# Other slots for the parts of two selective-scan layers, and a third buffer for `du`

## The chip, the cores and the metric

The kernel runs on one core of one Trainium2 chip. The metric is the device time of one execution in microseconds, lower is better; times are medians of several runs. Five queues issue the work: TensorE (PE; its weight loads are shown apart as PEld), VectorE (DVE), ScalarE (ACT), GpSimd (POOL) and SyncE (SP, which here issues nearly all DMAs). Each queue runs its instructions in the order in which the program wrote them, and instructions on different queues wait for each other through semaphores.

## The reference

Two layers follow each other on an image of 64 by 64 pixels and 192 channels, batch 8. Each normalises its input in groups, projects it to 384 channels for `x` and 384 for the gate `z`, applies a 3 by 3 depthwise convolution and SiLU, and runs a selective scan along the pixels in K directions (K = 2 in layer 0: rows forward and backward; K = 4 in layer 1: rows and columns, both ways). The sum over the directions is normalised over the channels, multiplied by the gate and projected back. Of each layer this matters:

```python
xs = ...                                              # [B, K, 384, 4096]
x_dbl = jnp.einsum('bkdl,kcd->bkcl', xs, x_proj_weight)
dts, Bs, Cs = jnp.split(x_dbl, [DT_RANK, DT_RANK + D_STATE], axis=2)
delta = jax.nn.softplus(jnp.einsum('bkrl,kdr->bkdl', dts, dt_projs_weight) + bias)
# for every pixel t, with 16 states n per channel:
#   h = exp(delta * A) * h + (delta * x) * B ;  y = sum_n h * C
y = (sum of the directions + x * Ds)
y = (y - mean) * rsqrt(var + eps) * ln_w + ln_b
out = einsum(y * act(z), out_proj_w)                  # act: gelu in layer 0, silu in layer 1
x = x + out
```

All arithmetic is float32.

## The kernel before

**Tiling.** The 384 channels are three tiles of 128 partitions (`DT` = 3, index `dt`), the 4096 pixels eight chunks of 512 (`T`). For each layer, `front` makes the convolved `x` of all images and leaves it in HBM; then `scans` does the rest. `scans` is what the change touches.

**Steps and slots.** A step `i` is one chunk of one direction `k` of one image: 128 steps in layer 0, 256 in layer 1. A step has 24 slots: slot `s` handles the state pair `m = s // 3` (two of the 16 states) and the channel tile `dt = s % 3`. In each slot the main loop writes, in this order:

- `scan` (L459): two hardware scans on DVE (L475), one for each state, which read `hb` from PSUM and `da`, and one multiplication of 1024 elements per partition on POOL, `hc = h * cr` (L476);
- the parts that a table `todo` holds for this slot;
- `inject(g + 2)` (L424): 8 matrix products that make `hb = delta * x * B` for the slot after the next. `hb` has two buffers of two PSUM banks each, so `inject(g + 2)` can start only when the scans of slot `g` have read theirs;
- `decay(g + 4)` (L444): two exponentials on ACT that make `da` for four slots on. `da` has five buffers, so this waits for the scans of slot `g - 1`.

So all queues are held to the pace of the scan pairs, PE two slots ahead and ACT four.

**The parts.** `at(i, s, f, ...)` puts part `f` at slot `s` of step `i`; numbers below 0 or above 23 fall in earlier or later steps. Within a slot, parts are sorted by `rank_of`: `f_keep`, then `f_act`, then the rest, then the products that use the buffer "m", then `reduce` and `add_y`, then loads. Three kinds of parts are put there.

- For the next step: `load_x`; in layer 1 `x_proj` (three products into `pd`) and `x_dbl`, in layer 0 `load_xdbl`; `turn_b` and `keep_b` (B is turned and sent to HBM); for each `dt`, `dt_proj` (PE, `pt`) and `dt_bias` (ACT, into `delta`); then `dt_softplus` (ACT, with a table load before and after it), and for each `dt` `make_du` (DVE, L383: `du = delta * x`, all operands in SBUF), `turn_du` (PE, `pq`) and `keep_du` (ACT).
- For the step itself: `load_b`, `load_c` (SP); `carry` (ACT); `reduce(m, n)` (PE: 12 products that add `hc` of one state to `py`); `load_y` or, where the direction changes from columns to rows, `load_turned` in 12 pieces; `add_y` (PE: 12 products that add y of the directions before); `keep_y` (ACT: copies `py` to SBUF, then five stores).
- For the chunks whose directions are all done, spread over K steps from step `e` on ("finish"): `f_norm`, `f_gate`, `f_keep` (the gate); `f_sum`, `f_keep_sum`, `f_all` (a mean over channels on PE, ACT, PE), `f_center` (DVE), `f_square` (ACT), the same three for the variance, `f_rstd` (ACT), `f_scale` (DVE), `f_act` (ACT), `f_affine` (ACT), `f_times` (POOL), `f_out` (PE), `f_add` (DVE), `f_store`. In layer 0, `e` is an odd step and the work covers that and the next (even) one; in layer 1 it covers four.

The last image's chunks can't wait for later steps; they get a denser order of their own in the last steps of a layer (`f_mean` in place of `f_sum` and `f_all`).

**One buffer for many.** PSUM has eight banks: four for `hb`, three for `py`, and one, the tag "m", which `pd`, `pb`, `pt`, `pq`, `pz`, `ps`, `pm` and `po` share. So a product that writes a new one of these waits until ACT or DVE has read the one before. In SBUF, `y` (for `load_y`, `load_turned` and the output of `keep_y`) has one buffer too, `du` has two, `h` two and `hc` and `cr` three.

Of the kernel before, what the change touches and what calls it, by code (L numbers as in the profile page):

```python
# [8 lines left out]
F32 = mybir.dt.float32  # L9
# [34 lines left out]
L0_ORDER = [1, 0]  # L44
L1_DIRS = [(True, False), (True, True), (False, True), (False, False)]
L1_ORDER = [1, 3, 2, 0]


def softplus(nc, out, in_):
# [200 lines left out]
            x_proj(*last)  # L250


def scans(tc, name, x_src, x_dst, xcd, xcd_col, xdd, t, dirs, rank, row_b, gate, consts, dram):

# [30 lines left out]
    with tc.tile_pool(name=f"{name}_s1", bufs=1) as s1, tc.tile_pool(  # L287
# [78 lines left out]

        def dt_bias(i, dt):
            k = steps[i][1]
            if dt == 0:
                live[i]["delta"] = s2.tile([P, DT, T], F32, name="delta")  # L370
            nc.scalar.activation(  # L371
                live[i]["delta"][:, dt], live[i]["pt"], AF.Identity, bias=dtb[:, k, dt : dt + 1]
            )
# [5 lines left out]

        def make_du(i, dt):  # L380

            du = s2.tile([P, T], F32, name="du")
            nc.vector.tensor_mul(  # L383
                du.rearrange("p (g r j) -> p r g j", r=2, j=G),
                live[i]["delta"][:, dt].rearrange("p (r g j) -> p r g j", r=2, j=G),
                live[i]["x"][:, dt].rearrange("p (r g j) -> p r g j", r=2, j=G),
            )
            live[i]["du", dt] = du
# [5 lines left out]
            live[i]["pq"] = pq  # L394

        def keep_du(i, dt):
            if dt == 0:
                live[i]["dut"] = s2.tile([P, DT, GC, P], F32, name="dut")
            nc.scalar.copy(live[i]["dut"][:, dt], live[i]["pq"])  # L399

# [145 lines left out]
        def f_norm(b, c):  # L546
            xn = s1.tile([P, DT, T], F32, name="xn_sq")
            fin["xn"] = xn[:CP, :CT]
            for u in range(CT):
                nc.scalar.activation(  # L550
                    fin["xn"][:, u],
                    fin["x"][:, u],
                    AF.Identity,
                    bias=t["gnb"][:, b, u : u + 1],
                    scale=t["grs"][:, b, u : u + 1],
                )
# [11 lines left out]
                )  # L568

        def f_keep(dt):  # L570
            if dt == 0:
                fin["g"] = s1.tile([P, DT, T], F32, name="g")
            nc.scalar.copy(fin["g"][:, dt], fin["pz"])

# [79 lines left out]
            )  # L654

        for i in range(N):
            j = i - 1  # L660
            at(j, -8, load_x, i)
            if xdd is None:
                for dt, s in enumerate((0, 1, 3)):
                    at(j, s, x_proj, i, dt)
                at(j, 4, x_dbl, i)
                b0, pts, act, d0 = 5, (6, 7, 9), 11, 13
            else:
                at(j, -4, load_xdbl, i)
                b0, pts, act, d0 = 2, (3, 4, 6), 9, 12
            at(j, b0, turn_b, i)  # L670
            at(j, b0 + 1, keep_b, i)
            for dt, s in enumerate(pts):
                at(j, s, dt_proj, i, dt)
                at(j, s + 1, dt_bias, i, dt)
            at(j, act, dt_softplus, i)
            for dt in range(DT):
                at(j, d0 + dt, make_du, i, dt)
                at(j, d0 + dt + 1, turn_du, i, dt)
                at(j, d0 + dt + 2, keep_du, i, dt)
            at(i, -12, load_b, i, 0)  # L680
            at(i, 0, load_b, i, 1)
            for m in range(NP):
                at(i, 3 * m - 6, load_c, i, m)
                at(i, 3 * m + 3, carry, i, m)
                for n in range(2):
                    at(i, 3 * m + 5 + n, reduce, i, m, n)
            b, k, cols, rev, ci, c = steps[i]
            if k and dirs[k - 1][0] != cols:
                for j in range(4 * DT):
                    at(i, 8 + j, load_turned, i, j)  # L690
                at(i, 24, add_y, i)
            else:
                at(i, 8, load_y, i)
                at(i, 15, add_y, i)
            at(i, 28, keep_y, i)

        def dealt(e, s, f, *a):

            for p, q in enumerate(s):
                at(e, q, f, *a, p)  # L700

        e = 0
        for b in range(B - 1):
            for c in range(NCH):
                e = max(e + K, (b + 1) * K * NCH - NCH + c + 1)
                if K == 2:
                    at(e, 0, f_load_x, b, c)
                    at(e, 6, f_load, b, c)
                    at(e, 6, f_norm, b, c)
                    for dt, s in enumerate(((7, 9), (16, 18), (19, 21))):  # L710
                        dealt(e, s, f_gate, dt)
                        at(e, s[1] + 1, f_keep, dt)
                    at(e, 22, f_sum, "y")
                    at(e, 23, f_keep_sum)
                    at(e, 24, f_all, "pm")
                    at(e, 25, f_center)
                    at(e, 26, f_square)
                    at(e + 1, 7, f_sum, "sq")
                    at(e + 1, 8, f_keep_sum)
                    at(e + 1, 10, f_all, "pv")  # L720
                    at(e + 1, 9, f_act)
                    at(e + 1, 11, f_rstd)
                    at(e + 1, 12, f_scale)
                    dealt(e + 1, (13, 14, 15), f_affine)
                    dealt(e + 1, (14, 15, 16), f_times)
                    for u, s in enumerate(((17, 18, 19), (20, 21, 22))):
                        dealt(e + 1, s, f_out, u)
                        at(e + 1, s[2] + 1, f_add, u)
                    at(e + 1, 23, f_store, b, c)
                else:  # L730
                    at(e, 0, f_load_x, b, c)
                    at(e, 6, f_load, b, c)
                    at(e, 8, f_norm, b, c)
                    for dt, s in enumerate(((10, 12), (18, 19), (21, 22))):
                        dealt(e, s, f_gate, dt)
                        at(e, s[1] + 1, f_keep, dt)
                    at(e + 1, 18, f_sum, "y")
                    at(e + 1, 19, f_keep_sum)
                    at(e + 1, 21, f_all, "pm")
                    at(e + 1, 22, f_center)  # L740
                    at(e + 1, 23, f_square)
                    at(e + 2, 11, f_act)
                    at(e + 2, 18, f_sum, "sq")
                    at(e + 2, 19, f_keep_sum)
                    at(e + 2, 21, f_all, "pv")
                    at(e + 2, 22, f_rstd)
                    at(e + 2, 23, f_scale)
                    dealt(e + 3, (6, 7, 8), f_affine)
                    dealt(e + 3, (7, 8, 9), f_times)
                    for u, s in enumerate(((10, 11, 12), (18, 19, 21))):  # L750
                        dealt(e + 3, s, f_out, u)
                        at(e + 3, s[2] + 1, f_add, u)
                    at(e + 3, 22, f_store, b, c)

        m0 = 10 if xdd is None else 7
        for c in range(NCH):
            b, e = B - 1, N - NCH + c + 1
            at(e, 5, f_load_x, b, c)
            at(e, 5, f_load, b, c)
            at(e, m0 + 4, f_norm, b, c)  # L760
            at(e, m0, f_mean, "y", "pm", 0, 1, 2)
            at(e, m0 + 1, f_center)
            at(e, m0 + 1, f_square)
            at(e, m0 + 2, f_mean, "sq", "pv", 0, 1, 2)
            at(e, m0 + 3, f_rstd)
            at(e, m0 + 4, f_scale)
            for dt in range(DT):
                at(e, m0 + 5, f_affine, dt)
                at(e, 17 + dt, f_gate, dt, 0, 1)
                at(e, 18 + dt, f_keep, dt)  # L770
                at(e, 20 + dt, f_times, dt)
            at(e, 20, f_act)
            for u in range(CT):
                at(e, 22 + u, f_out, u, 0, 1, 2)
                at(e, 23 + u, f_add, u)
            at(e, 24, f_store, b, c)

        rank_of = {
            f: r
# [23 lines left out]
                g += 1  # L803


def vss_layer(tc, name, x_src, x_dst, w, dirs, rank, row_b, gate, consts, dram):

    with ExitStack() as ctx:
        xcd, xcd_col, xdd, *dram = dram
# [3 lines left out]
            xcd_col = None  # L813
        t = load_weights(tc, ctx, name, w, len(dirs), rank, row_b + 2 * NS, consts[1])
        front(tc, name, x_src, xcd, xcd_col, xdd, t, consts)
        scans(tc, name, x_src, x_dst, xcd, xcd_col, xdd, t, dirs, rank, row_b, gate, consts, dram)


@with_exitstack
def two_vss_layers(ctx, tc, x, grp_d, w0, w1, out):  # L820
# [32 lines left out]
        for d in dgd:  # L853
            nc.sync.dma_start(out=d.rearrange("e (p x) -> (e p) x", p=P // 2), in_=zero)
    dram = (xcd, xcd_col, xdd, yrow, ycol, cscr, dgd)
    vss_layer(tc, "l0", x, mid, w0, L0_DIRS, 12, 32, AF.Gelu, consts, dram)
    vss_layer(tc, "l1", mid, out, w1, L1_DIRS, 96, 96, AF.Silu, consts, dram)


# [55 lines left out]
```

## Time and profile before

| | us |
|---|---|
| median of 3 runs | 27002.46 (26998.01 to 27004.6) |
| the profiled execution itself | 26994.35 |
| its span, from the first to the last instruction | 26992.1 |
| first scan and end of the scans of layer 0 | 1149.5 and 9797.8 |
| first scan and end of the scans of layer 1 | 10862.4 and 26916.4 |
| mean granted TensorE clock | 0.977 |

A page of the profile gives for each engine the time in which it was busy. A row of the costliest groups has the line, the engine, the operation, the tile written and the tiles read with their shapes and how often; then busy time in us and the mean of one in ns; then the idle time of the engine just before these instructions and what ended most of it. A timeline line has the start and the length in us, the engine, the line, what was written from what, and how many instructions were merged; in brackets the idle time before and what ended it. Lines with SPq are DMA issues on SyncE's queue: the length is that of the issue, the transfer lands later. Some groups that the change moves:

| line | what | count | mean ns |
|---|---|---|---|
| L434 | one of the 16 recorded products of an `inject` | 147456 | 289 |
| L451 | one exponential of `decay` | 18432 | 714 |
| L383 | `make_du` | 1152 | 887 |
| L50 | softplus over 1536 elements | 384 | 1485 |
| L524 | `keep_y` | 384 | 1439 |
| L633 | `f_times` | 384 | 1276 |
| L605, L616 | `f_center`, `f_scale` | 128 each | 1732, 1742 |
| L648 | `f_add` | 256 | 664 |

### The profile page before, as it was taken

What the parts mean: (1) busy time and instruction counts of PE and PEld (TensorE: products, weight loads), DVE (VectorE), ACT (ScalarE), POOL (GpSimd) and SP (SyncE); (2) the same over time, 40 slices, a digit from 0 to 9 for tenths busy, and PEclk for the clock granted to TensorE, in tenths of its full rate; (3) what the DMA queues carried; (4) which work ended last, traced back from release to release, by engine and by line L of the source; (5) the groups of instructions that cost most, each with busy time, mean ns of one, the idle gap of its engine ahead of it and who ended that gap; (6) DMA issues with size and microseconds to landing.
All of it is one profiled execution on the core that took longest, in us unless ns stands there. A gap on an engine that the chain in (4) does not pass through costs nothing.

```text
span 26992.1 us, 801807 instructions
## 1 busy us (share of the span) xinstructions
PE 24824.5 (92%) x348800; PEld 13646.4 (51%) x348800; DVE 23761.3 (88%) x21018; ACT 17601.2 (65%) x28132; POOL 23023.0 (85%) x9870
## 2 busy tenths in 40 slices
PE   9989999999999889899999999999999999999998
PEld 4455445454454444555555555555555555555554
DVE  2499999999999852899999999999999999999997
ACT  1266666666666642667677767777767767777765
POOL 2388888888888852899999999999999999999996
PEclk9999999999999999999999999999999999999999
DMA  2355555555555547555565565565565465565563
GB/s 93 103 143 145 144 144 146 143 146 147 145 146 146 138 117 131 147 146 149 147 147 147 149 148 147 151 147 150 147 148 150 146 146 150 148 145 151 150 145 113
DMA packets 4042222, 3838.88 MB, mean 142 GB/s; under 512 B 2519724, under 2 KB 2522564, under 8 KB 4038468
## 3 DMA queue, kind: packets, MB, share of 16 engines
q1 hardware_dynamic: 4035524, 3786.00, 53.7%
q8 instruction: 2764, 45.29, 0.7%
q14 instruction: 734, 6.01, 0.1%
q10 hardware_dynamic: 3200, 1.57, 0.0%
HBM read 3241.62 MB, written 545.33 MB: 140 GB/s over the span
## 4 chain that ended last, share of the span: by engine, by line
PE 38%; DVE 17%; issue 5%; ACT 3%; POOL 1%; DMA 0%; SPq 0%; DVEq 0%; ACTq 0%; POOLq 0%
PE hb L434 16%; DVE h L475 15%; PE py L57 10%; PE pt L358 3%; PE pd L310 3%; PE pc L57 2%; PE pz L562 1%; ACT da L451 1%; PE pi L176 1%; DVE du L383 1%; PE pq L393 1%; PE po L639 1%; POOL hc L476 0%; DVE yc L616 0%; ACT delta L50 0%
## 5 line engine op out<-in xcount | busy, mean ns | idle before, releaser
L476 POOL TENSOR_TENSOR hc<-h,cr 128x1024 f32<-128x1024 f32 x9216 | 22036.6, 2410 | 2706.0 <-DVE h L475 1752.8
L475 DVE TENSOR_TENSOR_SCAN h<-da,st,hb 128x512 f32<-128x512 f32 x16128 | 19244.9, 1258 | 1084.3 <-PE hb L434 936.1
L451 ACT ACTIVATE da<-delta,a_neg 128x512 f32<-128x512 f32 x18432 | 12164.8, 714 | 2242.6 <-DVE h L475 2228.8
L434 PEld LDWEIGHTS hb<-dg,dut 64*128 64x128 f32 x147456 | 9394.7, 188 | 8021.7 <-issue 7067.0
L434 PE MATMUL hb<-dg,dut 64*128 64x128 f32 x147456 | 11051.8, 289 | 1316.1 <-DVE h L475 1162.4
L57 PE MATMUL py<-hc,mask 32*32 32x512 f32 x147456 | 6982.8, 612 | 0.1
L475 DVE TENSOR_TENSOR_SCAN h<-da,hb 128x512 f32<-128x512 f32 x2304 | 2618.6, 1199 | 237.2 <-PE hb L434 226.2
L57 PEld LDWEIGHTS py<-hc,mask 32*32 32x32 f32 x147456 | 1273.1, 103 | 2353.8 <-issue 1983.6
L481 ACT COPY st<-h 128x6 f32<-128x6 f32 x2688 | 527.2, 196 | 1957.6 <-DVE h L475 1956.7
L162 POOL TENSOR_SCALAR xt<-xt,gm,grs 96x512 f32<-96x512 f32 x256 | 526.5, 2067 | 1118.6 <-DVE gsd L158 994.1
L358 PE MATMUL pt<-xdbl,w_dt 96*128 96x512 f32 (+1 forms) x2304 | 1316.6, 653 | 133.2 <-ACT delta L371 132.1
L371 ACT ACTIVATE delta<-pt,dtb 128x512 f32<-128x512 f32 x1152 | 792.2, 688 | 688.6 <-PE pt L358 685.6
L524 ACT COPY y<-py 128x1536 f32<-128x1536 f32 x384 | 552.5, 1439 | 962.5 <-PE py L57 962.5
L229 ACT ACTIVATE xo<-pc,cb 128x512 f32<-128x512 f32 x384 | 235.8, 684 | 1391.6 <-issue 1331.4
L393 PE MATMUL pq<-ident,du 128*128 128x128 f32 x4608 | 806.2, 301 | 348.6 <-DVE yc L616 146.4
L57 PE MATMUL pc<-pad,taps 32*32 32x512 f32 x27648 | 1097.1, 592 | 30.4 <-issue 30.3
L383 DVE TENSOR_TENSOR du<-delta,x_k 128x512 f32<-128x512 f32 x1152 | 1021.1, 887 | 71.7 <-ACT delta L50 70.4
L399 ACT COPY dut<-pq 128x512 f32<-128x512 f32 x1152 | 669.9, 581 | 545.0 <-PE pq L393 538.0
L183 DVE COPY pad<-pi 128x512 f32<-128x512 f32 x384 | 266.1, 693 | 860.6 <-PE pi L176 860.6
L639 PE MATMUL po<-yc,w_out 128*96 128x512 f32 x1536 | 865.1, 650 | 126.6 <-POOL yc L633 66.4
L310 PE MATMUL pd<-x_k,w_x 128*128 128x512 f32 x1536 | 876.9, 653 | 24.9 <-DVE yc L616 20.2
L562 PE MATMUL pz<-xn_sq,w_in 96*128 96x512 f32 x1536 | 864.9, 650 | 12.7 <-DVE yc L616 9.1
(90 smaller groups left out, 10100.8 us busy)
## 6 DMA issues: line engine op xcount, KB each, us to landing
cr<-cscr SPq DMA_DIRECT2D x2048, 512.0 KB, 3.9
dg<-dgd SPq DMA_DIRECT2D x1536, 512.0 KB, 7.3
cr<-xdd SPq DMA_DIRECT2D x1024, 512.0 KB, 5.5
x_k<-xcd SPq DMA_DIRECT2D x256, 768.0 KB, 7.4
xcd<-xo SPq DMA_DIRECT2D x128, 768.0 KB, 3.5
y<-yrow SPq DMA_DIRECT2D x128, 768.0 KB, 7.2
yc<-yrow SPq DMA_DIRECT2D x128, 768.0 KB, 5.3
x_k<-xcd_col SPq DMA_DIRECT2D x128, 768.0 KB, 6.0
```

The source lines that it names most:

```text
L57: nc.tensor.matmul(out[j * Q : (j + 1) * Q, dt], w[i * Q : (i + 1) * Q], x[i * Q : (i + 1) * Q], start=first, stop=last, tile_position=(i ...
L310: nc.tensor.matmul(live[i]["pd"][:R], w_x[:, dt, k, :], live[i]["x"][:, dt], start=(dt == 0), stop=(dt == DT - 1),)
L358: nc.tensor.matmul(pt, w_dt[:, k, dt * P : (dt + 1) * P], live[i]["xdbl"][:rank], start=True, stop=True,)
L371: nc.scalar.activation(live[i]["delta"][:, dt], live[i]["pt"], AF.Identity, bias=dtb[:, k, dt : dt + 1])
L383: nc.vector.tensor_mul(du.rearrange("p (g r j) -> p r g j", r=2, j=G), live[i]["delta"][:, dt].rearrange("p (r g j) -> p r g j", r=2, j=G) ...
L393: nc.tensor.transpose(pq[:, g], live[i]["du", dt][:, g * P : (g + 1) * P], ident)
L434: nc.tensor.matmul(hv[:, r, q], live[i]["dut"][r * G : (r + 1) * G, dt, q], dg[r * G : (r + 1) * G, q, :, 2 * mm : 2 * mm + 2], start=True ...
L451: nc.scalar.activation(da[:, n], live[i]["delta"][:, dt], AF.Exp, scale=a_neg[:, k, dt, 2 * m + n : 2 * m + n + 1],)
L475: nc.vector.tensor_tensor_scan(o, a, v, init, ALU.mult, ALU.add)
L476: nc.gpsimd.tensor_mul(hc[:, dt], h[:, dt], live[i]["cr", m])
L562: nc.tensor.matmul(fin["pz"], w_in[:, u, D + dt * P : D + (dt + 1) * P], fin["xn"][:, u], start=(u == 0), stop=(u == CT - 1),)
L639: nc.tensor.matmul(fin["po"][:CP], w_out[:, dt, u * CP : (u + 1) * CP], fin["y"][:, dt], start=(dt == 0), stop=(dt == DT - 1),)
```

## The change

The slot numbers, which stood in the code, move into four tables (`L0_SLOTS`, `L0_LAST`, `L1_SLOTS`, `L1_LAST`) that `vss_layer` hands to `scans`, and most of them change. No instruction is added or taken away, and no tile changes its size. Tuples are over `dt`, over the pieces of a product, or over the two sums (mean, variance). Before and after, as slots counted from the step `j = i - 1` for the next step's parts, from step `i` for its own, and from step `e` for the finish:

| part | layer 0 before | layer 0 after | layer 1 before | layer 1 after |
|---|---|---|---|---|
| x_proj, x_dbl | - | - | (0, 1, 3), 4 | (0, 1, 3), 4 |
| turn_b, keep_b | 2, 3 | 3, 4 | 5, 6 | 4, 5 |
| dt_proj | 3, 4, 6 | 4, 6, 0 | 6, 7, 9 | 10, 6, 8 |
| dt_bias | 4, 5, 7 | 5, 7, 2 | 7, 8, 10 | 11, 7, 9 |
| softplus | 9 | 7 | 11 | 11 |
| make_du | 12, 13, 14 | 9, 10, 15 | 13, 14, 15 | 13, 13, 13 |
| turn_du | 13, 14, 15 | 12, 13, 17 | 14, 15, 16 | 14, 15, 16 |
| keep_du | 14, 15, 16 | 13, 14, 18 | 15, 16, 17 | 15, 16, 17 |
| reduce (added to 3 m) | 5, 6 | 5, 5 | 5, 6 | 5, 6 |
| load_y, add_y | 8, 15 | 6, 10 | 8, 15 | 6, 14 |
| load_turned, add_y | - | - | 8 to 19, 24 | 8 to 19, 20 |
| keep_y | 28 | 28 | 28 | 29 |
| f_norm | 6 | 6 | 8 | 10 |
| f_gate | (7, 9), (16, 18), (19, 21) | (7, 10), (15, 15), (22, 22) | (10, 12), (18, 19), (21, 22) | (12, 12), (17, 19), (21, 23) |
| f_keep | 10, 19, 22 | 12, 17, 24 | 13, 20, 23 | 13, 21, 24 |
| f_sum, f_keep_sum, f_all (mean) | 22, 23, 24 | 18, 20, 20 | 42, 43, 45 | 36, 37, 46 |
| f_center, f_square | 25, 26 | 21, 24 | 46, 47 | 47, 54 |
| f_sum, f_keep_sum, f_all (variance) | 31, 32, 34 | 32, 33, 34 | 66, 67, 69 | 67, 70, 70 |
| f_act | 33 | 31 | 59 | 59 |
| f_rstd, f_scale | 35, 36 | 35, 35 | 70, 71 | 71, 71 |
| f_affine | 37, 38, 39 | 36, 37, 37 | 78, 79, 80 | 73, 73, 72 |
| f_times | 38, 39, 40 | 37, 37, 37 | 79, 80, 81 | 77, 76, 73 |
| f_out | (41, 42, 43), (44, 45, 46) | (39, 39, 39), (42, 45, 46) | (82, 83, 84), (90, 91, 93) | (84, 84, 84), (89, 91, 94) |
| f_add | 44, 47 | 40, 47 | 85, 94 | 85, 95 |

In the last steps, layer 0's finish starts a slot later (8 in place of 7 for the mean) and ends three earlier (`f_out` 19, 20 in place of 22, 23); layer 1's first half moves one slot earlier, its second half stays but for one `f_times`.

`du` gets three buffers. Since the parts of a step no longer come in the order of `dt`, the tiles `delta`, `dut` and `g` are allocated by whichever part comes first. The core of the diff, without the tables:

```diff
-            if dt == 0:
+            if "delta" not in live[i]:
                 live[i]["delta"] = s2.tile([P, DT, T], F32, name="delta")
...
-            du = s2.tile([P, T], F32, name="du")
+            du = s2.tile([P, T], F32, name="du", bufs=3)
...
-            if dt == 0:
+            if "dut" not in live[i]:
                 live[i]["dut"] = s2.tile([P, DT, GC, P], F32, name="dut")
...
             fin["xn"] = xn[:CP, :CT]
+            fin.pop("g", None)
...
-            if dt == 0:
+            if "g" not in fin:
                 fin["g"] = s1.tile([P, DT, T], F32, name="g")
...
+            at(j, slots["turn_b"], turn_b, i)
+            at(j, slots["keep_b"], keep_b, i)
             for dt in range(DT):
-                at(j, d0 + dt, make_du, i, dt)
-                at(j, d0 + dt + 1, turn_du, i, dt)
-                at(j, d0 + dt + 2, keep_du, i, dt)
+                for f in dt_proj, dt_bias, make_du, turn_du, keep_du:
+                    at(j, slots[f.__name__][dt], f, i, dt)
+            at(j, slots["softplus"], dt_softplus, i)
...
                 for n in range(2):
-                    at(i, 3 * m + 5 + n, reduce, i, m, n)
+                    at(i, 3 * m + slots["reduce"][n], reduce, i, m, n)
...
                 for j in range(4 * DT):
                     at(i, 8 + j, load_turned, i, j)
-                at(i, 24, add_y, i)
+                at(i, slots["add_turned"], add_y, i)
             else:
-                at(i, 8, load_y, i)
-                at(i, 15, add_y, i)
-            at(i, 28, keep_y, i)
+                at(i, 6, load_y, i)
+                at(i, slots["add_y"], add_y, i)
+            at(i, slots["keep_y"], keep_y, i)
```

## The prediction

> **What bounds the kernel now.** First the page: shares of the engines and the costliest groups.
>
> ```profile
> PE 24824.5 (92%) x348800; PEld 13646.4 (51%) x348800; DVE 23761.3 (88%) x21018; ACT 17601.2 (65%) x28132; POOL 23023.0 (85%) x9870
> L476 POOL TENSOR_TENSOR hc<-h,cr 128x1024 f32<-128x1024 f32 x9216 | 22036.6, 2410 | 2706.0 <-DVE h L475 1752.8
> L475 DVE TENSOR_TENSOR_SCAN h<-da,st,hb 128x512 f32<-128x512 f32 x16128 | 19244.9, 1258 | 1084.3 <-PE hb L434 936.1
> ```
>
> Three engines are nearly full, so no total decides; what counts is how long DVE waits in each slot (one pair of scans). Next the windows: an even and an odd step of layer 0, then the steady stage of each layer (stretch, length, busy PE, PEld, DVE, ACT, POOL, clock, DMA).
>
> ```profile
> 5145.06:5216.92 71.86, 64.28 (x860) 34.46 (x836) 63.77 (x57) 49.43 (x79) 61.47 (x28) 0.93 0.47 122
> 5216.92:5278.90 61.98, 57.35 (x844) 32.18 (x832) 58.97 (x53) 43.72 (x72) 56.98 (x24) 1.00 0.68 172
> 2727.00:9295.00 6568.00, 5972.23 (x81685) 3277.95 (x81684) 5977.75 (x5195) 4556.54 (x7209) 5806.10 (x2501) 0.96 0.56 145
> 12390.00:26327.00 13937.00, 13028.94 (x185220) 7233.08 (x185220) 13482.98 (x11604) 9810.85 (x15793) 12996.30 (x5524) 0.99 0.56 148
> ```
>
> DVE idles 590 us in the layer 0 stage (98 steps, 6.0 each) and 454 us in layer 1's (223 steps, 2.0 each). A better order can win no more than that: about 670 us over layer 0's 112 such steps, 500 over layer 1's. Last the timeline (start, length, engine, what), first where layer 0 loses time, then how `du` and `hc` meet in layer 1, then the SP queue before `add_y` of a step that turns y.
>
> ```profile
> 5157.41 1.44 ACT L524 COPY y<-py 128x1536 f32<-128x1536 f32 x1 [1.77 <-PE py L57]
> 5158.75 0.69 ACT L371 ACTIVATE delta<-pt,dtb 128x512 f32<-128x512 f32 x1
> 5159.49 1.12 PE L358 MATMUL pt<-xdbl,w_dt 12*128 12x512 f32 x2 [1.10 <-ACT delta L371]
> 5162.02 2.45 DVE L475 TENSOR_TENSOR_SCAN h<-da,st,hb 128x512 f32<-128x512 f32 x2 [1.06 <-PE hb L434]
> ...
> 15326.01 9.32 POOL L476 TENSOR_TENSOR hc<-h,cr 128x1024 f32<-128x1024 f32 x4
> 15330.16 5.73 DVE L383 TENSOR_TENSOR du<-delta,x_k 128x512 f32<-128x512 f32 x1
> ...
> 15578.45 12.58 POOL L476 TENSOR_TENSOR hc<-h,cr 128x1024 f32<-128x1024 f32 x5
> 15586.58 2.21 DVE L383 TENSOR_TENSOR du<-delta,x_k 128x512 f32<-128x512 f32 x1
> ...
> 15706.27 0.89 DVE L383 TENSOR_TENSOR du<-delta,x_k 128x512 f32<-128x512 f32 x1
> 15709.60 2.75 POOL L476 TENSOR_TENSOR hc<-h,cr 128x1024 f32<-128x1024 f32 x1 [0.20 <-DVE h L475]
> ...
> 15902.54 16.61 DVE L475 TENSOR_TENSOR_SCAN h<-da,st,hb 128x512 f32<-128x512 f32 x14
> 15908.69 5.41 SPq L508 DMA_DIRECT2D y<-ycol  x3
> 15915.19 0.43 SPq L508 DMA_DIRECT2D y<-ycol  x1
> 15925.70 1.30 PE L57 MATMUL py<-y,mask 32*32 32x512 f32 x8
> ```
>
> **Layer 0: waits that go.** The first four lines are slots 3 to 6. `dt_proj` 1 may write the one PSUM buffer "m" only after `dt_bias` 0, which stands on ACT behind `keep_y` (1.44), which waits for slot 3's `reduce`; so PE stands, `inject` is late and DVE waits 1.06. Such waits, added up in the timeline, cost slots 4 to 7 some 3.1 us in the even step, 1.8 in the odd. The new order puts the last `reduce` in slot 2, `dt_proj` 2 in slot 0 and 0 in slot 4, and only `keep_b` between `keep_y` and the next use of "m": ACT is through with `keep_y` and `keep_b` some 0.75 us before PE needs the buffer. Further on in the even step DVE waits 0.9 for `f_rstd` before `f_scale`, then 0.6 and 1.4 behind ACT and PE, then 1.1 and 0.8 where `f_out` shares slots with `reduce`.
>
> What PE loses by load alone goes by one rule, read from the timeline. An `inject` starts 0.23 us after its scan pair ends, takes 1.08, and may start 0.8 later before DVE waits; a pair takes 2.34. Other PE work: `reduce` 1.05, pt, pd, pz, pm 1.06, po 1.03, pq 0.59, ps 0.99, `add_y` 1.26. A slot with `reduce`, one pt and `inject` is 3.19, 0.85 too much: that is the wait of 0.45 found in layer 1's slots 4, 10 and 22. Summed slot by slot, load makes 4.2 us per pair of steps before and 2.1 after: both `reduce`s now share a slot, but the slots on either side are free, and the fullest (20: 3.14 beside `inject`) stands before `f_center`, whose 1.65 on DVE covers it. ACT's burst (`f_act` 2.8, `softplus` with its two table loads 4.1) now starts in slot 7, so `f_all` waits about 1.2 for `f_keep_sum` behind it and `f_scale` some 0.5 for `f_rstd`. The three `f_times` in slot 13 put POOL 3.7 late, and `du` 2 in slot 15 meets that: 0.4 to 1.6 if it gets in at the next end of a POOL instruction, 6.2 if only when POOL has run dry. I take 1.2, as the short POOL runs behind. Waits after: 2.1 + 0.5 + 1.2 = 3.8 per pair, against 11.1 in the two windows and 12.0 over the stage; 56 pairs, **-450** (-300 to -520).
>
> **Layer 1: PE load.** The same sum per four steps (one finished chunk) is 4.8 before, 2.8 after: pt leaves slot 9 for slot 10, where no `reduce` is, and slots 12 and 14 with 3 to 4 us of PE work lie beside the three `du` of slot 13. With the ratio of measured to summed waits (1.2): 0.6 per step, 248 steps, **-150** (-220 to 0).
>
> **Three `du` in one slot.** Alone in its slot a `du` has a pitch of 0.58; the first takes 0.89, as it waits 0.25 for the running `hc`, and the `hc` that meets a `du` takes 2.75 instead of 2.37. So the two don't run together. Two `du` in a row, with an `hc` waiting, never occur in the trace. From below: they keep together, and cost what they cost apart (0). From above: `hc` gets in after the first, and the second waits 2.36 with the scans behind it. The nearest rows are those where one waits while the other has a next instruction queued: at 15586.58 `du` waited 1.64 and got in though POOL's five `hc` follow without a gap, and in nearly every step it gets in with `hc` 13 queued; at 15330.16 it waited for all that POOL had (5.7). I take the first kind: who waits gets in. So slot 13 becomes 2.3 longer, and 0.25 of PE wait per step goes with it: 200 steps, **+400** (0 to 460). In every fourth step (56) POOL comes to slot 13 some 3.4 late from `f_times` in slots 1 to 5, with eight and more `hc` in a row; either kind then gives 6 us of wait, where slots 13 to 15 lose 3.3 now: **+150** (-100 to 170).
>
> The Trainium skill, "SBUF — State Buffer", section "Who interferes with whom", says that a VectorE instruction with two SBUF inputs contends with a GpSimd instruction that reads SBUF, and "Issue order, not op shape, decides who blocks". It speaks against this change: `hc` is issued before the second `du`. By it the sum is the forecast below; it leaves the 5.73 at 15330.16 unexplained.
>
> **`add_y` of turned steps in slot 20.** In 64 steps y comes in 12 pieces, issued in slots 8 to 19, unmoved. Seven pairs from 15902.54 are slots 16 to 22, so slot 20 begins at 15912.0; the last piece is issued at 15915.19 and such pieces land after 4.5 (median of line 508, 3.3 to 8.9): 15919.7. In slot 24 PE came later than that. In slot 20 PE arrives at 15914.3 and stands 5.4 us, with `inject` for slot 22 behind it and DVE behind that. DVE loses 4.7, and 0.8 to 1.8 more as PE meets slots 21 to 23 without slack; the 1.9 that `add_y` costs in slot 24 (this step 62.5 against 60.6 four steps earlier) goes: +4.5. Pieces are paced by SP and the DMA rings, so a slot 13 that is 2.3 longer takes that off: +2.2 each, **+140** (0 to 350).
>
> **Moved at no cost.** `load_y` (slot 6) waits on SP for the stores of `keep_y`; behind it stand `f_load` and one `load_c`, needed six slots later. `keep_y` in slot 29 is done on ACT about 0.8 us before `reduce` needs py. The third `du` buffer frees the first for slot 12; no row shows a wait on it. In the last seven steps of each layer only layer 0's order gets denser: **-30**.
>
> **Sum.** -450 -150 +400 +150 +140 -30 = +60; against the profiled execution's 26994.35 (span 26992.1): 27,054; the median of the runs shown is 8 higher: 27,060.
>
> **Rivals.** (1) The three `du` stay together: no +400, +150 falls to 0, `add_y` costs 290: -340, 26,660. For it: back-to-back DVE instructions overlap by 0.08, so no gap may open; against it, the many rows where the waiting engine gets in. It decides if `hc` cuts in in fewer than some 160 of 200 steps. (2) Layer 0's `du` 2 waits until POOL is dry: 4.6 more, 56 times, 27,320. For it the 5.73; against it, that came after long runs of `hc`. (3) The last piece lands in time, as SP gets ahead of stalled scans: 26,900; for it 3.3 as the least landing.
>
> **Numbers.** Forecast 0.52, own range 26,880 to 27,330; (1) 0.29, 26,550 to 26,850; (2) 0.13; (3) 0.06. 0.2% is 54 us, about what a measurement of this kernel can tell from no change. Faster: 0.08 of the forecast's 0.52, 0.28 of (1), 0.04 of (3): 0.40. Within: 0.12 from the forecast and 0.01 from (1). Slower: 0.32, 0.13 and 0.02: 0.47. The range takes in (1) and most of (2): 26,580 to 27,380.
>
> **What would show it.** Slot 13 of layer 1: one `du` of about 2.9 with an `hc` before it (right) or three at 0.6 (rival 1). `add_y` of turned steps: PE waiting on `y<-ycol`, some 250 us in all. Layer 0 pairs near 125 us against 133.8, no ACT wait ahead of pt; `du` of slot 15 above 2.5 us means rival 2. It is wrong altogether if ACT's burst in slot 7 makes `decay` late, so that scans wait for `da`.

## The result, and the profile after

The changed kernel takes 27,332.81 us (median of 4 runs, 27,302.92 to 27,352.2) against 27,003.53 for the one before (4 runs): a ratio of 1.0121, with a 95% interval of 1.0103 to 1.0138. It is slower by some 330 us; the forecast was 27,060, slower by 60. The profiled execution has a span of 27,300.6 us.

First the page of the changed kernel: shares of the engines and the groups that answer to those shown before.

```profile
PE 25004.3 (92%) x348800; PEld 13936.9 (51%) x348800; DVE 24483.1 (90%) x21018; ACT 17681.9 (65%) x28133; POOL 22806.8 (84%) x9870
L569 POOL TENSOR_TENSOR hc<-h,cr 128x1024 f32<-128x1024 f32 x9216 | 21790.0, 2387 | 3245.2 <-DVE h L568 2754.6
L568 DVE TENSOR_TENSOR_SCAN h<-da,st,hb 128x512 f32<-128x512 f32 x16128 | 19146.9, 1257 | 828.8 <-PE hb L527 790.3
L476 DVE TENSOR_TENSOR du<-delta,x_k 128x512 f32<-128x512 f32 x1152 | 1773.0, 1573 | 70.6 <-ACT delta L143 53.1
```

The scans of the third line stand idle less than before (828.8 us against 1084.3, most of it for `hb`), and yet DVE is busy for 722 us more. The last line accounts for all of it. Before, it was:

```profile
L383 DVE TENSOR_TENSOR du<-delta,x_k 128x512 f32<-128x512 f32 x1152 | 1021.1, 887 | 71.7 <-ACT delta L50 70.4 <-PE pq L393 1.2
```

The 1152 `du` took 1021 us and take 1773 now. A `du` that waits for an `hc` to end counts as busy, so this is waiting, too. The windows, over the same steps as those shown before, say where (an even and an odd step of layer 0, then the steady stage of each layer; columns as before).

```profile
4954.56:5017.51 62.95, 58.85 (x857) 34.23 (x845) 62.07 (x55) 48.95 (x78) 59.90 (x28) 1.00 0.55 136
5017.51:5082.34 64.83, 60.06 (x839) 35.40 (x834) 63.26 (x54) 44.14 (x72) 57.93 (x25) 0.97 0.69 169
2662.00:8916.78 6254.78, 5816.52 (x81684) 3392.77 (x81683) 6105.43 (x5194) 4558.24 (x7209) 5780.75 (x2502) 0.99 0.59 152
12052.70:26596.60 14543.90, 13377.26 (x185189) 7367.70 (x185168) 13979.72 (x11603) 9877.72 (x15786) 12827.94 (x5523) 0.97 0.53 142
```

Layer 0's even step went from 71.86 to 62.95 us, its stage from 6568.0 to 6254.8. But the odd step got longer, 61.98 to 64.83. Layer 1's stage grew from 13,937.0 to 14,543.9: the loss lies there, and the granted TensorE clock in it fell from 0.99 to 0.97, a first hint that TensorE stood still more often.

Step by step, from both traces: the time of a slot runs from the start of its scans to the start of the next slot's, in us. Where steps differ, the number is their mean. A step that turns y adds the y of columns in a step of rows (64 steps); every fourth step is one with the `f_times` of a finish.

| place | before | after | steps |
|---|---|---|---|
| layer 0, pair of steps | 134.3 | 127.7 | 56 pairs |
| its odd step, slot 9 | 2.3 | 5.9 | |
| layer 1, ordinary step, slots 13 to 15 | 9.04 | 11.3 | some 190 |
| ... slot 16, where y isn't turned | 2.4 | 2.34 in 49 steps, 3.2 to 4.8 in 83 | 132 counted |
| layer 1, every fourth step, slots 13 to 15 | 12.6 | 16.9 | 56 |
| layer 1, step that turns y, slot 21 | 2.3 | 6.2 | 64 |

Where nothing is late a slot takes 2.34 us.

**Slot 13.** The view of one line, `du`, in one ordinary step's slot 13 (shortest, median and longest in ns, then first and last start), and below it the timeline from there on.

```profile
L476 DVE TENSOR_TENSOR du<-delta,x_k x3: 679/875/2862, 18450.5 to 18454.1; 128x512 f32<-128x512 f32 x3
```

```profile
18453.32 1.33 PE L150 MATMUL py<-y,mask 32*32 32x512 f32 x24
18457.26 1.21 PE L527 MATMUL hb<-dg,dut 64*128 64x128 f32 x16 [2.62 <-DVE h L568]
18459.45 1.99 PE L150 MATMUL py<-hc,mask 32*32 32x512 f32 x24
...
18462.83 2.45 DVE L568 TENSOR_TENSOR_SCAN h<-da,st,hb 128x512 f32<-128x512 f32 x2 [1.03 <-PE hb L527]
```

The first `du` takes 0.88, the second 2.86, the third 0.68: between the first and the second POOL's next `hc` got in, as the forecast had it. What it did not have comes after. TensorE stands 2.62 us, as no scan frees `hb`. Its next `reduce` (24 recorded products, 12 in the program) takes 1.99 instead of 1.11 us, and the scans after slot 16 wait 1.03 for `hb`. Another ordinary step has the same stall and none of this: its nine scans run without a wait.

```profile
17654.32 1.20 PE L527 MATMUL hb<-dg,dut 64*128 64x128 f32 x16 [2.61 <-DVE h L568]
...
17651.74 10.64 DVE L568 TENSOR_TENSOR_SCAN h<-da,st,hb 128x512 f32<-128x512 f32 x9
```

The windows tell the two apart. The first two are of the first step (from slot 12 to 13's end, then 3.45 us after the stall), the third is the 3.45 us after the stall of the other; the clock is the third number from the end:

```profile
18445.81:18454.68 8.87, 7.78 (x148) 4.33 (x124) 8.87 (x9) 8.81 (x13) 7.78 (x4) 1.00 0.57 155
18457.30:18460.75 3.45, 3.45 (x44) 1.92 (x44) 3.45 (x4) 2.97 (x7) 3.32 (x2) 0.65 0.08 15
17654.36:17657.81 3.45, 3.45 (x56) 2.31 (x58) 3.45 (x4) 2.85 (x5) 3.34 (x2) 1.00 0.11 17
```

In the first step TensorE was granted 0.65 of its clock after it had stood still, at the moment when it had the most to catch up on; in the other it kept its full clock. So it is in the whole trace. In the 132 ordinary steps that don't turn y, TensorE stands 2.0 to 2.9 us in these slots. In 83 a stretch of lower clock follows, and slot 16 takes 3.2 to 4.8 us. In 49 none follows, and it takes 2.34 or 2.35. The Trainium skill, "TensorE: Matmul & The Clock Gate", section "Why this matters for your kernels", sets the limit at idle gaps of about 3 us; here a gap of 2.6 was followed by the lower clock, and the measurement decides. What does tell the two kinds of stall apart stands in the last section.

**Every fourth step.** POOL and the `du` of such a step, in the timeline:

```profile
15352.83 1.29 POOL L727 TENSOR_TENSOR yc<-yc,g 128x512 f32<-128x512 f32 x1
15354.06 18.62 POOL L569 TENSOR_TENSOR hc<-h,cr 128x1024 f32<-128x1024 f32 x8
...
15366.75 7.69 DVE L476 TENSOR_TENSOR du<-delta,x_k 128x512 f32<-128x512 f32 x3
```

The three `f_times` (the last at 15352.83) have put POOL behind the scans. The first `du` is called at 15366.75 and holds DVE 6.5 us, to just past the end of POOL's run (15354.06 + 18.62 = 15372.68). The other two take 0.68 each. How far POOL is behind can be counted: scan pairs that are finished while their `hc` hasn't begun, when a `du` is called. In the whole trace, with one such pair the median `du` that doesn't follow another takes 0.86 us (52 of 523 took more than 2.5, all of them in the slot of the next case); of the 113 that met two or three, 57 took more than 2.5, all eight that met three among them (median 7.5).

**Layer 0's odd step, slot 9** shows the same thing in small: a single finished pair waits there, but its `hc` gets in before the `du`, which takes 3.67.

```profile
5041.17 3.67 DVE L476 TENSOR_TENSOR du<-delta,x_k 128x512 f32<-128x512 f32 x1
```

**A step that turns y.** The timeline about slot 21: the last of the 12 pieces is issued, and `add_y` (L150, `py<-y`) runs in two parts.

```profile
19956.62 0.43 SPq L601 DMA_DIRECT2D y<-ycol  x1
19957.46 2.22 PE L150 MATMUL py<-y,mask 32*32 32x512 f32 x16
19960.70 2.01 PE L150 MATMUL py<-y,mask 32*32 32x512 f32 x8 [1.02 <-DMA y<-ycol]
...
19963.95 3.62 DVE L568 TENSOR_TENSOR_SCAN h<-da,st,hb 128x512 f32<-128x512 f32 x3 [3.96 <-PE hb L527]
```

The scans lose 3.96 us, though TensorE waits only 1.02 for the DMA. The products take the rest: 2.22 us for 16 recorded ones and then 2.01 for 8 at a granted clock of 1.00, where an ordinary step does all 24 in 1.33 (line 18453.32 above).

### The profile page after: what moved, and what is told of

Read it like the earlier page. It is cut to its first block, busy times and chain, and to the rows that moved or that the text cites. A ratio compares the mean times of both kernels' runs of the same rounds, so it can differ in the third digit from the quotient of the medians.

```text
span 27300.6 us, 800813 instructions
## 1 busy us (share of the span) xinstructions
PE 25004.3 (92%) x348800; PEld 13936.9 (51%) x348800; DVE 24483.1 (90%) x21018; ACT 17681.9 (65%) x28133; POOL 22806.8 (84%) x9870
## 4 chain that ended last, share of the span: by engine, by line
DVE 29%; PE 22%; issue 9%; DMA 2%; ACT 2%; POOL 1%; SPq 1%; DVEq 0%; ACTq 0%; POOLq 0%
DVE h L568 25%; PE hb L527 8%; PE py L150 6%; DVE du L476 3%; PE pc L150 2%; PE pd L403 2%; PE pi L269 1%; PE pq L486 1%; PE pz L656 1%; POOL hc L569 1%; DMA y<-ycol 1%; ACT da L544 1%; PE po L733 0%; SPq L601 0%; DVE yc L710 0%
## 5 line engine op out<-in xcount | busy, mean ns | idle before, releaser
L569 POOL TENSOR_TENSOR hc<-h,cr 128x1024 f32<-128x1024 f32 x9216 | 21790.0, 2387 | 3245.2 <-DVE h L568 2754.6
L568 DVE TENSOR_TENSOR_SCAN h<-da,st,hb 128x512 f32<-128x512 f32 x16128 | 19146.9, 1257 | 828.8 <-PE hb L527 790.3
L150 PE MATMUL py<-hc,mask 32*32 32x512 f32 x147456 | 7046.5, 617 | 2.7 <-POOL hc L569 2.7
L150 PEld LDWEIGHTS py<-hc,mask 32*32 32x32 f32 x147456 | 1584.3, 104 | 2394.3 <-issue 1869.8
L568 DVE TENSOR_TENSOR_SCAN h<-da,hb 128x512 f32<-128x512 f32 x2304 | 2603.0, 1198 | 164.3 <-PE hb L527 158.5
L476 DVE TENSOR_TENSOR du<-delta,x_k 128x512 f32<-128x512 f32 x1152 | 1773.0, 1573 | 70.6 <-ACT delta L143 53.1
L150 PE MATMUL pc<-pad,taps 32*32 32x512 f32 x27648 | 1093.9, 590 | 30.1 <-issue 30.1
L150 PEld LDWEIGHTS pc<-pad,taps 32*32 32x32 f32 x27648 | 627.9, 103 | 477.8 <-issue 298.9
L733 PE MATMUL po<-yc,w_out 128*96 128x512 f32 x1536 | 797.6, 624 | 63.5 <-POOL yc L727 36.8
```

The source lines that it names most:

```text
L150: nc.tensor.matmul(out[j * Q : (j + 1) * Q, dt], w[i * Q : (i + 1) * Q], x[i * Q : (i + 1) * Q], start=first, stop=last, tile_position=(i ...
L476: nc.vector.tensor_mul(du.rearrange("p (g r j) -> p r g j", r=2, j=G), live[i]["delta"][:, dt].rearrange("p (r g j) -> p r g j", r=2, j=G) ...
L568: nc.vector.tensor_tensor_scan(o, a, v, init, ALU.mult, ALU.add)
L569: nc.gpsimd.tensor_mul(hc[:, dt], h[:, dt], live[i]["cr", m])
L733: nc.tensor.matmul(fin["po"][:CP], w_out[:, dt, u * CP : (u + 1) * CP], fin["y"][:, dt], start=(dt == 0), stop=(dt == DT - 1),)
```

## The experiments

**One (e1): the three `du` apart again.**

```diff
-    "make_du": (13, 13, 13),
+    "make_du": (13, 14, 15),
```

> The changed kernel with make_du of layer 1 back in slots 13, 14, 15. Theory (an hc that waits takes the gap between two du): slots 13 to 15 of an ordinary layer 1 step go from 11.2 us back to about 9.1, those of every fourth step from 17.2 to some 13; du of about 2.9 us vanish. Against that, the wait of add_y in turned steps grows by about 2 us each, as the long slot 13 covered part of it. Net about -400: 26,930 us (26,800 to 27,050). Rival (layer 1's loss is PE load and the half clock after idling, and du only shows it): the steps keep their length, 27,250 to 27,400.

Measured: 26,856.87 us, ratio to the kernel before 0.9952 (0.9936 to 0.9969). This one row of a table turns the loss into a gain, and the rival is out. Ordinary steps have 9.1 us in slots 13 to 15 again and lose nothing in slot 16. But steps that turn y wait longer now, as their slot 20 comes sooner:

```profile
19621.92 2.03 PE L150 MATMUL py<-y,mask 32*32 32x512 f32 x8 [5.21 <-DMA y<-ycol]
19623.88 1.88 PE L527 MATMUL hb<-dg,dut 64*128 64x128 f32 x16
```

TensorE stands 5.21 us for the last piece, and its next `inject` takes 1.88 instead of 1.20. Slot 21 loses about 8 us here (5 in every fourth step), some 4 in the changed kernel. So the stall in slot 13 had been hiding part of the landing.

**Two (e2): `add_y` of steps that turn y in slot 24, alone.**

```diff
-    "add_turned": 20,
+    "add_turned": 24,
```

> The changed kernel with add_y of turned steps of layer 1 back in slot 24. Theory (PE stands in slot 20 until the last of 12 pieces has landed): the idle time of 3 to 4.5 us in slot 21 of the 64 turned steps vanishes, some 2 us come back in slot 1 of the next step: -2.3 each, about -150: 27,180 us (27,080 to 27,260). PE's waits on y<-ycol vanish from the list. Rival (the transfers themselves set the length of those steps, wherever add_y stands): within 50 us of 27,330.

Measured: 27,132.62 us, 1.0052 (1.0037 to 1.0067), as expected; TensorE no longer waits for `y<-ycol`.

**Three (e3): both.**

> Both at once. Theory: du costs go as in the run with du apart, and the turned steps lose only the 2 us of slot 1, so the two together bring more than the sum of each alone: about -650 from the changed kernel, 26,680 us (26,560 to 26,800). If the two were independent: the sum of the two single gains, about -550.

Measured: 26,436.66 us, 0.9796 (0.9781 to 0.981), 240 better than expected. By the ratios to the kernel before, the two edits alone bring some 460 and 190 us, together 880. Each had taken the other's gain: `add_y` in slot 20 costs 420 us where nothing hides the landing (one against three) and 190 behind the stall of slot 13 (the change against two).

**Four (e4): layer 0's new order, layer 1's old one.** All of layer 1's table goes back but `load_y` and the third buffer.

```diff
-    "dt_proj": (10, 6, 8),
-    "make_du": (13, 13, 13),
-    "add_turned": 20,
+    "dt_proj": (6, 7, 9),
+    "make_du": (13, 14, 15),
+    "add_turned": 24,
...
```

> Layer 0 as changed, layer 1 in its old slots (all but load_y, which stays at 6; du with three buffers). Theory (the whole loss is layer 1's, and layer 0 gains what its scans show, 409 us): 26,600 us (26,540 to 26,660), ratio about 0.985. Rival (part of layer 0's gain is shifted into layer 1, or the changed load_y costs): over 26,700.

Measured: 26,570.26 us, 0.9846 (0.9832 to 0.9861). So layer 0's part is worth about 416 us, and the rest of layer 1's new order (three against four) 134. Layer 1 itself takes as long as before the change, so `load_y` and the third buffer cost and win nothing there.

**Five (e5): the kernel before with layer 1's three `du` in slot 13.**

```diff
-            du = s2.tile([P, T], F32, name="du")
+            du = s2.tile([P, T], F32, name="du", bufs=3)
...
-                at(j, d0 + dt, make_du, i, dt)
+                at(j, d0 if xdd is None else d0 + dt, make_du, i, dt)
```

> The kernel before with only this: make_du of layer 1 in slots 13, 13, 13, and three buffers of du. Theory: hc takes the gap after the first du of each step, so slots 13 to 15 go from 9.1 to 11.2 us in the ordinary steps, with du of 0.9, 2.9 and 0.7: +2.1 in some 200 steps and 2 to 4 in the 56 others, 27,480 us (27,380 to 27,650). Rival (the three du cost only together with the new PE order): below 27,150.

Measured, in a single run: 28,047.82 us against 26,995.28, so +1,050 where +485 was expected. The expectation was wrong by more than its range. The timeline of TensorE and DVE from slot 15 on of an ordinary step:

```profile
18997.03 1.36 PE L434 MATMUL hb<-dg,dut 64*128 64x128 f32 x16 [3.71 <-DVE h L475]
18999.37 1.99 PE L57 MATMUL py<-hc,mask 32*32 32x512 f32 x24
19001.07 1.38 PE L57 MATMUL py<-y,mask 32*32 32x512 f32 x24
...
19003.69 1.28 DVE L475 TENSOR_TENSOR_SCAN h<-da,st,hb 128x512 f32<-128x512 f32 x1 [2.12 <-PE hb L434]
```

Slots 13 to 15 lose what was expected (9.06 to 11.3), and slot 16 as much again: 4.9 us instead of 2.4. TensorE stands 3.71, then meets a `reduce` and `add_y` of slot 15 before `inject`, at a clock of 0.63 in the first 3.41 us. In the changed kernel `add_y` is in slot 14 and is done in the stall itself. The next run tests that.

**Six (e11): as five, with `add_y` in slot 14.**

```diff
-                at(i, 15, add_y, i)
+                at(i, 14 if xdd is None else 15, add_y, i)
```

> The kernel of e5 with layer 1's add_y (of the steps that don't turn) in slot 14 instead of 15. In e5's trace TensorE stands 3.7 us for slot 13's three du and then does the products of slots 15 and 16 at a lower granted clock, the 24 of add_y (1.38 us) among them; slot 16 waits 2.5 us for inject. Theory: what made e5 600 us costlier than expected is this load behind the stall; add_y in slot 14 is done while VectorE stands and takes its 1.4 us out of it: 190 steps by 1.4 to 1.7 us, about -300, 27,750 us (27,650 to 27,850), slot 16 at 3.2 to 3.6 us as in the kernel after. Rival: slot 16 waits for the clock and the du chain alone, whatever lies in it: 28,050 as e5.

Measured, in a single run: 27,735.59 us against 26,978.71: +757, 295 less than five. In the 132 ordinary steps that don't turn y, slot 16 falls from 4.9 to 3.0 us on average. The rival falls, as the work queued behind the stall counts, but the theory is only half of it: the two traces show the clock's share. In five the stall is 3.7 us, a stretch of lower clock follows it in all 132 steps, and slot 16 takes 4.0 to 5.8. In six `add_y` fills a part of the stall and leaves 2.6. Lower clock follows in 75 steps, with 3.5 us in slot 16 on average, and not in 57, where it takes 2.34 or 2.35. So `add_y` in the stall saves twice: less work is left for the slow stretch, and fewer stretches are slow. What five's load would cost at the full clock, no run shows.

**Seven (e7): the kernel before with `add_y` of steps that turn y in slot 20.**

```diff
-                at(i, 24, add_y, i)
+                at(i, 20, add_y, i)
```

> The kernel before with only this: add_y of turned steps of layer 1 in slot 20. Theory: nothing covers the wait for the last piece now, so slot 21 idles about 8 us as in the run with du apart, and 2.2 us of slot 1 go: +5.5 in 64 steps, 27,350 us (27,250 to 27,450). Rival (the wait comes from the changed order of the loads before it): below 27,150.

Measured, in a single run: 27,412.12 us (+417), inside the range; the rival is out. Without the stall of slot 13 this edit costs 6.5 us in each of 64 steps.

**Eight (e8): layer 0 without `f_times`.** This leaves out the multiplication with the gate in layer 0, so its time shows what those products cost there and not what a whole kernel could take.

```diff
         def f_times(dt):
+            if xdd is not None:
+                return
```

> The changed kernel without f_times in layer 0 (the gate isn't multiplied there). Theory (the three products in slot 13 of the even step leave POOL late up to slot 9 of the odd one, where du then waits 3 us for it): slot 9 of the odd step falls from 5.7 to about 2.9, slots 15 and 16 of the even one by 0.5 together; 56 pairs, -180: 27,140 us (27,080 to 27,200). Rival (du of slot 9 waits for softplus or for x): slot 9 stays, within 40 us of 27,320.

Measured, in a single run: 27,102.99 us, 230 below the changed kernel. The odd step's slot 9 falls from 5.9 to 3.2 us on average and its `du` to 0.8 in the median. Those products run on POOL one step earlier, and nothing in the odd step itself had changed.

**Nine (e9): as three, `add_y` one slot later.**

```diff
-    "add_turned": 24,
+    "add_turned": 25,
```

> The kernel of e3 with the additions of the turned steps one slot later again (25, that is slot 1 of the next step, where VectorE has no reduction). Theory: the 64 turned steps still stand about 1.7 us at the additions, since the products of y finish on GpSimd only in the next step's first slots; one slot later takes that wait away: 56 to 64 steps by 1.5 to 1.9 us, about -100, 26,340 us (26,290 to 26,400). Rival: the wait moves with the additions (GpSimd's products start later, not the additions too early): 26,440 as e3.

Measured: 26,438.97 us, 0.9797 (0.9783 to 0.9812), the same as three. The rival holds, but the reason given there for either is wrong: nothing on GpSimd is waited for. By then every piece has landed, and the wait moves because the 24 products themselves take 2.25 us in the timeline, one block without a wait:

```profile
19487.72 2.25 PE L150 MATMUL py<-y,mask 32*32 32x512 f32 x24
```

**Ten (e10): as nine, `f_times` on DVE.** In the last steps it stays on POOL.

```diff
-    "f_times": (37, 37, 37),
+    "f_times": (36, 37, 38),
...
-        def f_times(dt):
-            nc.gpsimd.tensor_mul(fin["y"][:, dt], fin["y"][:, dt], fin["g"][:, dt])
+        def f_times(dt, eng=nc.vector):
+            eng.tensor_mul(fin["y"][:, dt], fin["y"][:, dt], fin["g"][:, dt])
...
-                at(e, last["f_times"][dt], f_times, dt)
+                at(e, last["f_times"][dt], f_times, dt, nc.gpsimd)
```

> The kernel of e9 with the three products with the gate (f_times) of the main finish on VectorE instead of GpSimd, in layer 0 in slots 36, 37 and 38; in the last steps they stay on GpSimd. Theory: GpSimd is then no longer late where the du come, so the wait in slot 13 of layer 1's every fourth step falls from 9 to about 3.5 us and slot 9 of layer 0's odd step from 5.7 to 2.9 us; the products cost VectorE about 0.6 us each. By that (60 steps by 3.5) + (60 pairs by 1.2) = -280, 26,060 us (25,900 to 26,250). Rival: the long waits come from hc's length alone and not from the three products ahead of it: then only the cost shows, about +200, 26,540 us.

Measured: 26,103.14 us, 0.9673 (0.9657 to 0.9689), the fastest of all: 3.3% below the kernel before. It is inside the range, and the rival is out. The group of `du` on its page and the timeline of an every-fourth step's slot 13:

```profile
L476 DVE TENSOR_TENSOR du<-delta,x_k 128x512 f32<-128x512 f32 x1152 | 866.7, 753 | 70.5 <-ACT delta L143 70.5
...
14914.13 19.31 POOL L569 TENSOR_TENSOR hc<-h,cr 128x1024 f32<-128x1024 f32 x8 [0.38 <-DVE h L568]
14930.33 0.88 DVE L476 TENSOR_TENSOR du<-delta,x_k 128x512 f32<-128x512 f32 x1
```

DVE has 336 products more, of 0.67 us each in the median, and gains more than it pays: the mean `du` falls to 753 ns (887 before the change, 1169 in three). The run of eight `hc` is as long as the one shown of the changed kernel, but it started right after its scans ([0.38 <-DVE h L568]), and the `du` takes 0.88: what counts is not the length of a run but how late POOL is in it. In this trace no `du` meets more than one finished pair without its `hc`; in three 105 did, and 46 of them took more than 2.5 us. In every fourth step slot 13 falls from 9.2 to 4.5 us, slot 9 of layer 0's odd step from 5.9 to 3.2.

## Why the prediction was right or wrong

The runs give each term its measured size. Differences are those of the ratios, by 27,000 us; the parts are added in this order, since they are not independent. The traces split off every fourth step: its slots 13 to 15 get longer by 137 us from four to three, by 73 from three to two and by 27 from two to the change, which the rows beside it leave out.

| term | forecast | measured | from |
|---|---|---|---|
| layer 0, with its last steps | -480 | -416 | four against before |
| layer 1, TensorE's load | -150 | about -270 | three against four (-134) |
| three `du` in a slot, ordinary steps | +400 | about +620 | two against three (+690) |
| every fourth step, slots 13 to 15 | +150 | about +240 | the three pairs of traces |
| `add_y` of turned steps in slot 20 | +140 | about +160 | the change against two (+190) |
| sum | +60 | +330 | |

The direction was right, every term has the right sign, and the time lies in the stated range, though 3 us above the forecast's own one (26,880 to 27,330). But the two `du` terms came out larger, and a larger gain in TensorE's load hid a part of that. The step that failed most is "So slot 13 becomes 2.3 longer, and 0.25 of PE wait per step goes with it".

**Three `du`.** Its first half is right: 2.86 for a `du` with an `hc` before it, slots 13 to 15 longer by 2.2 (some 190 steps, about 430 us). Rival 1, that they stay together, is out: `hc` cut in in all 191 ordinary steps. But the relief for TensorE was a cost. After the stall it loses clock in most steps and does the products behind it late, and slot 16 waits: 0.9 to 2.4 us in the ordinary steps with lower clock and nothing in the others, some 180 us in all with the turned steps, where the forecast took off 50. Five and six show that the work placed behind the stall, too, sets this price.

**Every fourth step.** Slots 13 to 15 went from 12.6 to 16.9 us, 56 times, instead of the +150. More than half of it comes without three `du` in a slot: in three they take 15.1. There the first `du` of slot 13 takes over 2.5 us in 53 of the 56 steps, in four in 29. Ten shows that it is POOL's lateness from `f_times`: with these on DVE the slots take 10.3. Which of the moved slots made the lateness worse was not tested.

The rule of the Trainium skill that the prediction weighs, "Issue order, not op shape, decides who blocks" ("SBUF — State Buffer", "Who interferes with whom"), agrees with the 2.86: `hc` was waiting before the second `du` came up. It does not settle the 6.5 at 15366.75, where POOL began two more `hc` while `du` waited, nor the 56 of 113 that met the same lateness and took less; how the turn is given then stays open.

**Layer 0.** The even step gained as forecast: no ACT wait ahead of `pt` is left. `du` of slot 15 takes at most 1.4 us, so rival 2 is false in its place; that its 27,320 lies near the result is chance. But the cause it named, POOL late from three `f_times` in one slot, was paid for in the next step's slot 9, which the forecast put at no cost. Eight shows it: without `f_times` that wait is gone and 230 us with it, some 150 of them in that slot. Pairs stand at 127.7 instead of near 125, which is about the 64 us of the table.

**TensorE's load.** Right in sign, and larger than forecast: the other slots of layer 1 lose some 270 us from four to three. The -134 of the run looks like the -150 only because every fourth step takes 137 back. In the change as it is, slot 16 takes another 180.

**`add_y` in slot 20.** The size came out near, by other parts than the forecast's. TensorE was to wait "some 250 us in all" for `y<-ycol`. The view of that transfer, who waited for it, in the changed kernel and then in one:

```profile
  PE py L150: 44.8, 43
```

```profile
  PE py L150: 222.0, 64
```

So rival 3 is half true: behind the stall the last piece lands almost in time. The price was in the products, which the forecast's list of TensorE's work has at 1.26 for an `add_y`: once the last piece is late they run in two parts of 2.22 and 2.01 us. And had the `du` been apart, the 222 us and the lower clock after them would have made it 420. A step forecast as a sum of independent terms thus came near for a wrong reason.

**Last steps.** Layer 0's last seven went from 580 to 551 us, as forecast; layer 1's from 562 to 597, most of it by the same three `du`: with them apart (three) it is 569. Two of the `f_times` there moved a slot earlier, not one, as the list of the change has it.

## What to carry to other kernels

A stall on the engine that sets the pace is not paid when it ends: look which engine it leaves idle, what that engine has queued behind it, and at which clock it will do it. Move into the stall what can be done there: it shortens the queue behind and the idle time. Two instructions that exclude each other (`du` and `hc` here) are cheap while neither is late. So keep them apart by a slot each, and take other work off the engine that comes late to the meeting, even where the busier engine does it instead (ten). Two edits can hide each other's cost: undo them one by one and together before either is judged.

## What the runs showed of the hardware

- Two `du` in a row lose the gap between them to a waiting `hc` (0.88, 2.86, 0.68 us). A `du` that meets POOL two or three `hc` behind can take until POOL has caught up (5 to 7.5 us), and did each of the 8 times when it was three.
- TensorE's granted clock was 0.65 in the 3.45 us after a stall of 2.6 us and 0.63 after one of 3.7; 24 recorded `reduce` products took 1.99 instead of 1.11 us. These are means: the trace's clock record has only 1 and 0.5, and the 0.5 starts and ends on a fixed grid of 3.41 us. What counts is how much of the idle time falls into one stretch of that grid. In all twelve traces, away from start and end, a stretch at full clock in which TensorE idled for more than 2.1 us was followed by one at 0.5 in 1,491 of 1,491 cases (155 of them in the changed kernel), one with less than 0.6 us in 6 of 66,108; in between both occur. Of the stall before 18457.26, 2.36 us fall into one stretch; the grid cuts the one before 17654.32 into 1.06 and 1.55, and the clock stays.
- The products of a turned `y` read it in steps of 8 elements, the only difference to other steps that the code shows. 24 recorded ones take 2.25 us against 1.33, and 16 or 8 of them take nearly as long as 24 (2.22, 2.01): a split `add_y` is paid twice. The Trainium skill, "SBUF — State Buffer", the note on SBUF cachelines, has a penalty for accesses that cross 16-byte lines, which fits with it; no run here changed the step alone.
